# Transposing attention probabilities on VectorE and by DMA instead of on TensorE, in two stages of a four-layer kernel

## The chip, the cores and the metric

The kernel runs on one core of a Trainium2 chip. The core has five engines with an instruction queue each: TensorE (in the profile PE, with its weight loads as PEld), VectorE (DVE), ScalarE (ACT), GpSimd (POOL) and SyncE (SP), which here does nothing but issue DMAs. Sixteen DMA engines move the data. An engine takes its instructions in order, and an instruction whose operands are not ready holds up all that is queued behind it on that engine. The metric is device time in microseconds (us) for one launch of the whole kernel.

## The reference, cut to what matters

The program is four transformer layers on 1024 tokens of width 256, each an attention and a feed-forward part. The change touches the second and the fourth attention (L1 and L3 in the names of the inputs, `attn1` and `attn3` in the kernel). Both compute, for 16 heads of width 128 and in float32:

```
q, k, v = projections of x                      # L1: 16 heads each; L3: 16 query heads, 4 key/value heads
                                                # L3 also normalizes each q and k row by its mean square
s = q @ k.T * scale                             # 1024 x 1024 scores of a head
s = where(col <= row, s, -inf)                  # causal
p = softmax(s)
out = concat over heads (p @ v) @ Wo            # added to x, then normalized
```

The feed-forward part of the third layer (L2) has weights packed in 4 bits. The kernel unpacks them while `attn1` runs, and that unpacking is touched as well.

## The kernel before, in words

**Blocks.** The 1024 tokens are 8 blocks of P = 128. A *unit* is one head and one block of 128 queries. With the causal mask, query block j needs key blocks 0 to j, so a unit has 1 to 8 blocks of 128 keys, 4.5 on average. Each of the two attentions has 128 units and 576 squares of 128 x 128 probabilities.

**The loops.** `attn1` goes over four groups g of four heads, in a group over the heads h, in a head over half (0, 1) and s (0 to 3): the units of a head have 1, 2, ... 8 blocks. `attn3` goes over four groups g, in a group over the query block b (0 to 7), in a block over the four heads h: four units of equal size follow each other. Between units both stages work off a list of `pieces`, which are the projections that make queries, keys and values of this group and the next; in the last group few or none are left.

**A unit's way through the engines.** `scores` (L277) multiplies queries by keys on TensorE (L281) into a PSUM tile called `wide`, of which there are two. `exp_scores` (L237) adds the mask to the last 128 columns on VectorE (L241), takes the maximum of the row on VectorE (L246; in `attn3` one more small multiplication, L248) and the exponential on ScalarE with the sum of the row beside it (L251). `norm_probs` (L257) inverts the sum on VectorE (L258) and scales the row on GpSimd (L259). `transpose_probs` (L261) transposes each 128 x 128 square on TensorE into a PSUM bank (L268), and ScalarE copies up to four squares at a time to the SBUF tiles `pt` (L272). The product with the values, in `attend` (L1042 in `attn1`, L1934 in `attn3`), takes a value block as the stationary side and 512 columns of `pt`, that is four units, as the moving side (L1047, L1937). VectorE copies its result out (L1054, L1944), and the output projection follows (L1032 in `attn1`, L701 in `attn3`).

**The order around the change.** Both stages run under `in_order` (L140): PE, ACT, DVE and POOL execute their instructions in the order in which the Python code emits them. SP is not among these, so its DMAs go out as soon as a buffer is free. The order is made by `Pipe.advance` (L394), which is called once for each new unit i. It emits, in this order: `norm_probs` of unit i-1; what stands in `k.later` (GpSimd operations of the unpacking); `scores` of unit i; `transpose_probs` of unit i-2; `exp_scores` of unit i; then one step of the products with values that are due. `Pipe.then` (L390) makes a product due three calls after its last unit was handed in. After that the stage's loop emits pieces and a step of the unpacking.

**Buffers.** `SCOPES` (L2033) gives the number of buffers of each pool: in `attn1` three for the exponentials (`p4`) and three for the transposed (`pt`, 128 x 4 x 512), in `attn3` three and four. PSUM has eight banks; two `wide` tiles take four, the rest is the pool `bank`.

**Loads.** `load(g)` in `attn1` (L949) issues the weights of the next group at the second unit of a group, in `attn3` (L1759) at its fifth. `ffn2_weights` (L1680) loads packed weights and scales on SP (L1690 to L1704), unpacks them on VectorE in steps (`dequantize`, L1640; L1651 is its first operation) and on GpSimd (L1672, L1673), and stores the result on SP (L1711).

Of the kernel before, what the change touches and what calls it, by code (L numbers as in the profile page):

```python
# [31 lines left out]
P = 128  # L32
T = 1024
NT = T // P
D = 256
# [7 lines left out]
class Kit:  # L43
# [96 lines left out]
    def in_order(self):  # L140

        e = mybir.EngineType
        return self.tc.manual_schedule(engines={e.PE, e.Activation, e.DVE, e.Pool})
# [117 lines left out]
    def transpose_probs(self, probs, blocks, pts, slot):  # L261


        for lo in range(0, blocks, 4):
            n = min(4, blocks - lo)
            ps = self.bank()
            for i in range(n):
                self.nc.tensor.transpose(  # L268
                    ps[:, i * P : (i + 1) * P],
                    probs[:, (lo + i) * P : (lo + i + 1) * P], self.ident,  # L270
                )
            self.nc.scalar.copy(  # L272
                pts[lo // 4][:, :n, slot * P : (slot + 1) * P],
                ps[:, : n * P].rearrange("p (b q) -> p b q", b=n),
            )

# [101 lines left out]
class Pipe:  # L378
# [3 lines left out]


    def __init__(self, k):
        self.k, self.first, self.second, self.rest, self.queued = k, None, None, [], []

    def unit(self, query, key, blocks, pts, slot, scale=None):
        self.advance((query, key, blocks, pts, slot, scale))
# [5 lines left out]
    def advance(self, new=None):  # L394
        k = self.k
        if self.first:
            k.norm_probs(*self.first[:3])
        k.catch_up()
        if new:
            query, key, blocks, pts, slot, scale = new  # L400
            sc = k.scores(query, key, blocks * P)
        if self.second:
            probs, n, _, pts_, slot_ = self.second
            k.transpose_probs(probs, n // P, pts_, slot_)
        self.second = self.first
        self.first = None
        if new:
            probs, inv = k.exp_scores(sc, blocks * P, scale)
            self.first = (probs, blocks * P, inv, pts, slot)
# [4 lines left out]
        while self.rest and next(self.rest[0], self) is self:  # L414
            self.rest.pop(0)

    def busy(self):
        return self.first or self.second or self.queued or self.rest
# [518 lines left out]
def attn1(k, a):  # L937


    nc = k.nc  # L940
    scale = 1.0 / math.sqrt(128)
# [7 lines left out]
    def load(g):  # L949
        cols = slice(g * 512, (g + 1) * 512)  # L950
        wk, wv = (
            k.weights([P, NC, 512], a[n][:, cols].rearrange("(c p) f -> p c f", p=P))
# [1182 lines left out]
```

## Time and profile before

| what | value |
|---|---|
| median of three runs | 2349.58 us (2348.33 to 2350.21) |
| profiled execution, its own time | 2349.2 us |
| its span, first to last instruction | 2347.5 us |
| granted TensorE clock, mean | 0.976 of full speed |
| window of the second attention's units | about 441 to 960 us, then its last output projections |
| window of the fourth attention's units | about 1480 to 1966 us |
| VectorE transposes, copies from SBUF to SBUF by SP in these windows | none |

The page gives for each engine the busy time, a share of the span and a count of instructions. Busy time is an average over eight stages, so the two attentions are looked at in windows of their own. The chain of work that ended last is followed backwards from the last instruction; what a line has of it is time that the line really set. In the groups of instructions a row reads: line, engine, operation, written tile <- read tiles, shapes, count | busy us, mean ns of one | idle time of the engine before them, and what ended it. A line number is that of the code printed above.

### The profile page before, as it was taken

The page shows a single profiled execution, that of the slowest core. Times are in us where ns is not written, and L with a number is a line of the kernel's source. Part 1 is how long each engine was busy: PE and PEld are TensorE (multiplying, and loading weights), DVE is VectorE, ACT ScalarE, POOL GpSimd, SP SyncE. Part 2 cuts the span into 40 slices and gives each one's busy share as a digit, 9 for nine tenths or more (in the row PEclk, how much of TensorE's full clock was granted, in tenths as well). Part 3 has the DMA queues.
Part 4 walks back from the last instruction along what each step waited for, and adds up shares of the span by engine and source line. Part 5 has one row for each costly group of instructions (what it writes and reads, how often), then busy time and mean ns, then how long its engine had stood idle before and what let it go on. Part 6 is the DMA issues. An engine that isn't in the chain of part 4 may idle for free.

```text
span 2347.5 us, 25446 instructions
## 1 busy us (share of the span) xinstructions
PE 2168.4 (92%) x8563; PEld 1222.0 (52%) x8563; DVE 1228.8 (52%) x2799; ACT 913.7 (39%) x2358; POOL 492.8 (21%) x637
## 2 busy tenths in 40 slices
PE   7999768899999999988898999899999999999997
PEld 4666544566656665754444444455555554444443
DVE  5677556565655646555773445544445575222223
ACT  3666524434343435444453223454445442111111
POOL 4333221322222323321110000332222221000000
PEclk9999979999999999989999999999999999999998
DMA  5100163110111101013200001000000000101100
GB/s 169 35 12 25 44 198 111 38 49 24 46 36 59 45 29 40 19 54 97 76 2 10 27 28 45 9 1 19 1 18 10 10 1 18 36 28 54 30 1 18
DMA packets 59346, 92.24 MB, mean 39 GB/s; under 512 B 9072, under 2 KB 33712, under 8 KB 59216
## 3 DMA queue, kind: packets, MB, share of 16 engines
q1 hardware_dynamic: 54304, 78.15, 10.4%
q0 software_dynamic: 4912, 12.46, 1.9%
q8 instruction: 69, 1.13, 0.2%
q14 instruction: 61, 0.50, 0.1%
HBM read 69.76 MB, written 17.17 MB: 37 GB/s over the span
## 4 chain that ended last, share of the span: by engine, by line
PE 68%; issue 11%; DVE 10%; ACT 6%; DMA 2%; POOL 1%; SPq 1%; DVEq 0%; ACTq 0%; POOLq 0%
PE bank L152 18%; PE wide L281 9%; PE bank L1047 5%; PE wide L306 5%; PE bank L268 5%; PE bank L1937 4%; PE bank L159 3%; ACT e L635 3%; PE bank L701 3%; PE bank L1032 2%; PE bank L1464 1%; PE bank L881 1%; PE bank L1202 1%; DVE st L627 1%; PE bank L690 1%
## 5 line engine op out<-in xcount | busy, mean ns | idle before, releaser
L152 PE MATMUL bank<-xT,w 128*128 128x512 f32 (+2 forms) x1520 | 659.0, 563 | 3.5 <-DVE xT L178 2.6
L152 PEld LDWEIGHTS bank<-xT,w 128*128 128x128 f32 (+1 forms) x1520 | 285.7, 193 | 279.9 <-issue 256.0
L259 POOL TENSOR_SCALAR p<-p,st 128x128 f32<-128x128 f32 (+7 forms) x256 | 190.9, 746 | 672.5 <-DVE st L258 530.9
L272 ACT COPY pt<-bank 128x512 f32<-128x512 f32 (+3 forms) x384 | 171.0, 480 | 316.4 <-PE bank L268 313.4
L281 PE MATMUL wide<-k,q 128*128 128x512 f32 (+3 forms) x768 | 290.6, 487 | 3.7 <-ACT p L251 2.8
L281 PEld LDWEIGHTS wide<-k,q 128*128 128x128 f32 x768 | 142.1, 190 | 136.6 <-issue 121.3
L246 DVE TENSOR_REDUCE st<-wide 128x1 f32<-128x128 f32 (+7 forms) x256 | 194.1, 758 | 13.5 <-DVE wide L241 0.5
L306 PE MATMUL wide<-t,w 128*128 128x512 f32 (+1 forms) x392 | 188.5, 603 | 4.9 <-DVE t L2026 3.2
L268 PE MATMUL bank<-ident,p 128*128 128x128 f32 x1152 | 169.3, 274 | 21.4 <-POOL p L259 20.0
L268 PEld LDWEIGHTS bank<-ident,p 128*128 128x128 f32 x1152 | 137.7, 141 | 85.6 <-issue 39.0
L2025 DVE TENSOR_TENSOR t<-t,bank 128x512 f32<-128x512 f32 (+1 forms) x66 | 45.4, 687 | 249.5 <-PE bank L152 248.9
L2024 ACT ACTIVATE t<-bank 128x512 f32<-128x512 f32 (+1 forms) x66 | 39.4, 597 | 315.1 <-PE bank L152 315.1
L241 DVE TENSOR_TENSOR wide<-wide,causal 128x128 f32<-128x128 f32 x256 | 74.7, 292 | 125.9 <-PE wide L281 124.8
L1047 PE MATMUL bank<-pt,v 128*128 128x512 f32 (+3 forms) x384 | 139.4, 487 | 0.0
L1937 PE MATMUL bank<-pt,v 128*128 128x512 f32 x288 | 137.4, 596 | 0.0
L251 ACT ACTIVATE p<-wide,st,factor 128x128 f32<-128x128 f32 (+7 forms) x128 | 106.4, 831 | 73.7 <-DVE st L248 73.0
L306 PEld LDWEIGHTS wide<-t,w 128*128 128x128 f32 (+1 forms) x392 | 68.3, 189 | 109.4 <-issue 48.0
L159 PE MATMUL bank<-w,xT 128*128 128x512 f32 (+3 forms) x320 | 122.8, 521 | 1.7 <-DVE xT L178 0.9
L251 ACT ACTIVATE p<-wide,st 128x128 f32<-128x128 f32 (+7 forms) x128 | 95.0, 742 | 65.2 <-DVE st L246 64.6
L635 ACT ACTIVATE e<-wide,st 128x128 f32<-128x128 f32 x256 | 89.8, 377 | 51.4 <-DVE st L627 36.2
L1489 ACT ACTIVATE pt<-wide 128x1024 f32<-128x1024 f32 (+3 forms) x96 | 75.6, 810 | 70.4 <-PE wide L1483 68.6
L233 DVE TENSOR_TENSOR x<-bank,x 128x256 f32<-128x256 f32 x120 | 49.6, 422 | 92.6 <-PE bank L1032 34.5
(309 smaller groups left out, 3066.7 us busy)
## 6 DMA issues: line engine op xcount, KB each, us to landing
w<-in_L_ffn_gate_up_dram SPq DMA_DIRECT2D x16, 512.0 KB
w<-in_L_attn_Wq_dram SPq DMA_DIRECT2D x12, 512.0 KB
w<-in_L_attn_Wo_dram SPq DMA_DIRECT2D x12, 512.0 KB
rows<-parts SPq DMA_DIRECT2D x16, 256.0 KB
w<-in_L_ffn_down_dram SPq DMA_DIRECT2D x8, 512.0 KB
w<-in_L_attn_Wk_dram SPq DMA_DIRECT2D x7, 512.0 KB
w<-in_L_attn_Wv_dram SPq DMA_DIRECT2D x6, 512.0 KB
moe_results<-y SPq DMA_DIRECT2D x23, 128.0 KB
```

Source lines behind the costliest of these rows:

```text
L152: self.nc.tensor.matmul(out, lhsT=weight(c), rhs=self.xcols(c, lo, n), start=c == 0, stop=c == NC - 1)
L159: self.nc.tensor.matmul(out, lhsT=self.xcols(c, lo, n), rhs=weight(c), start=c == 0, stop=c == NC - 1)
L246: nc.vector.tensor_reduce(top, scores[:, :n], axis=AX.X, op=ALU.max, negate=True)
L251: nc.scalar.activation(probs[:, :n], scores[:, :n], AF.Exp, bias=top, scale=1.0 if scale is None else scale, accum_out=total,)
L259: self.nc.gpsimd.tensor_scalar(probs[:, :n], probs[:, :n], total, 1.0, ALU.mult, ALU.mult)
L268: self.nc.tensor.transpose(ps[:, i * P : (i + 1) * P], probs[:, (lo + i) * P : (lo + i + 1) * P], self.ident,)
L272: self.nc.scalar.copy(pts[lo // 4][:, :n, slot * P : (slot + 1) * P], ps[:, : n * P].rearrange("p (b q) -> p b q", b=n),)
L281: self.nc.tensor.matmul(s[:, lo : lo + m], lhsT=query, rhs=key(lo, m), start=True, stop=True)
L306: nc.tensor.matmul(acc[m][:, half * HALF : (half + 1) * HALF], lhsT=down[:, m * P : (m + 1) * P], rhs=h, start=i == 0, stop=i == count - 1,)
L635: nc.scalar.activation(e[:, r, f, b, :], sc[:, r, f, b, :], AF.Exp, bias=top[:, at : at + 1], accum_out=total[:, at : at + 1],)
L1047: nc.tensor.matmul(out[:, lo:], lhsT=values[g, b][:, h * P : (h + 1) * P], rhs=pts[b // 4][:, b % 4, lo:], start=b == 0, stop=b == 4 * hal ...
L1937: nc.tensor.matmul(out, lhsT=values[i][:, g * P : (g + 1) * P], rhs=pts[i // 4][:, i % 4, :], start=i == 0, stop=i == b,)
```

## The change

The transposition is done in two steps without TensorE and PSUM. VectorE transposes squares of 32 x 32 within a row of partitions: `turn_probs` is one VectorE instruction for a whole unit, which reads the probabilities with a step of four elements (16 bytes) and writes densely into a new pool `turned` (two buffers). Four DMAs on SP, one for each 32 partitions of queries, then move rows of 128 to 1024 bytes from `turned` to their partitions in `pt`. What lands in `pt` has the 128 keys of a block on partitions, permuted consistently, and the queries in eight segments of 32 for two units.

A `pt` tile now serves two units (a *pair*) instead of four. The product with the values therefore has 256 moving columns instead of 512, and twice as many matmuls; its result is copied out by ScalarE instead of VectorE. In `attn1` only the last block of a pair is cut to 128 columns.

`Pipe.advance` has one stage less: it emits `norm_probs` of unit i-1, `scores` and `exp_scores` of unit i, and then `turn_probs` of unit i-1. A product still becomes due three calls after its last unit; when two or more products are waiting, two of them get a step.

SP joins the engines whose order is the code's (`in_order(transfers=True)`). The load of the next group in `attn1` is spread over three units, eight units later than before. In `attn1` all queries are copied out of PSUM by ScalarE, where VectorE did it for groups 1 to 3 (L985). Loads and stores of the unpacking move from SP's queue to GpSimd's; that part of the code comes at the same place, and so the load of the next packed tile is issued in the same step as the first operation on it.

```diff
-    def in_order(self):
+    def in_order(self, transfers=False):
         e = mybir.EngineType
-        return self.tc.manual_schedule(engines={e.PE, e.Activation, e.DVE, e.Pool})
+        engines = {e.PE, e.Activation, e.DVE, e.Pool}
+        return self.tc.manual_schedule(engines=engines | {e.SP} if transfers else engines)
...
-    def transpose_probs(self, probs, blocks, pts, slot):
-        for lo in range(0, blocks, 4):
-            n = min(4, blocks - lo)
-            ps = self.bank()
-            for i in range(n):
-                self.nc.tensor.transpose(
-                    ps[:, i * P : (i + 1) * P],
-                    probs[:, (lo + i) * P : (lo + i + 1) * P], self.ident,
-                )
-            self.nc.scalar.copy(
-                pts[lo // 4][:, :n, slot * P : (slot + 1) * P],
-                ps[:, : n * P].rearrange("p (b q) -> p b q", b=n),
-            )
+    def turn_probs(self, probs, blocks, pt, slot):
+        nc = self.nc
+        n = blocks * P
+        turned = self.tile("turned", [P, 2 * HALF])
+        nc.vector.transpose(
+            turned[:, :n].rearrange("p (b k q) -> p b k q", b=4, q=32),
+            probs[:, :n].rearrange("p (k i b) -> p b k i", b=4, i=32),
+        )
+        for a in range(4):
+            nc.sync.dma_start(
+                out=pt[:, slot * 4 + a, : blocks * 32],
+                in_=turned[a * 32 : a * 32 + 32, :n].rearrange("i (b r) -> i b r", b=4),
+            )
+    def probs_tile(self, blocks):
+        n = 4 if blocks <= 4 else 8
+        return self.tile("pt", [P, 8, n * 32], tag=f"pt{n}", bufs=self.pt_bufs[n])
+    def values(self, out, value, pt, b, last, first=0):
+        self.nc.tensor.matmul(
+            out[:, first * P :].rearrange("p (s q) -> p s q", q=32), lhsT=value,
+            rhs=pt[:, first * 4 :, b * 32 : b * 32 + 32], start=b == 0, stop=last,
+        )
...
-    def unit(self, query, key, blocks, pts, slot, scale=None):
-        self.advance((query, key, blocks, pts, slot, scale))
+        self.k, self.first, self.rest, self.queued = k, None, [], []
+    def unit(self, query, key, blocks, pt, slot, scale=None):
+        self.advance((query, key, blocks, pt, slot, scale))
     def then(self, steps):
@@ -393,29 +408,28 @@
     def advance(self, new=None):
         k = self.k
-        if self.first:
-            k.norm_probs(*self.first[:3])
+        before, self.first = self.first, None
+        if before:
+            k.norm_probs(*before[:3])
         k.catch_up()
         if new:
-            query, key, blocks, pts, slot, scale = new
+            query, key, blocks, pt, slot, scale = new
             sc = k.scores(query, key, blocks * P)
-        if self.second:
-            probs, n, _, pts_, slot_ = self.second
-            k.transpose_probs(probs, n // P, pts_, slot_)
-        self.second = self.first
-        self.first = None
-        if new:
             probs, inv = k.exp_scores(sc, blocks * P, scale)
-            self.first = (probs, blocks * P, inv, pts, slot)
+            self.first = (probs, blocks * P, inv, pt, slot)
+        if before:
+            probs, n, _, pt, slot = before
+            k.turn_probs(probs, n // P, pt, slot)
         for q in self.queued:
             q[0] -= 1
         while self.queued and self.queued[0][0] <= 0:
             self.rest.append(self.queued.pop(0)[1])
-        while self.rest and next(self.rest[0], self) is self:
-            self.rest.pop(0)
+        for _ in range(min(2, len(self.rest))):
+            while self.rest and next(self.rest[0], self) is self:
+                self.rest.pop(0)
...
+    k.pt_bufs = {4: 2, 8: 2}
...
-        if g == 0:
-            nc.scalar.activation(
-                out, ps, AF.Identity, bias=scaled_bq[:, j : j + 1], scale=scale
-            )
-        else:
-            nc.vector.tensor_scalar(out, ps, bq[:, j : j + 1], scale, ALU.add, ALU.mult)
+        nc.scalar.activation(out, ps, AF.Identity, bias=scaled_bq[:, j : j + 1], scale=scale)
...
-    def attend(g, h, half, pts):
-        out = k.bank()
-        for b in range(4 * half + 4):
-            lo = max(0, b - 4 * half) * P
-            nc.tensor.matmul(
-                out[:, lo:], lhsT=values[g, b][:, h * P : (h + 1) * P],
-                rhs=pts[b // 4][:, b % 4, lo:], start=b == 0, stop=b == 4 * half + 3,
-            )
-            if b % 2:
+    def attend(g, h, half, pair, pt):
+        count = 4 * half + 2 * pair + 2
+        out = k.bank()[:, : 2 * P]
+        for b in range(count):
+            last = b == count - 1
+            k.values(out, values[g, b][:, h * P : (h + 1) * P], pt, b, last, int(last))
+            if b % 4 == 3 and not last:
                 yield
-        oT = outs[g, h, half] = k.tile("ot", [P, HALF])
-        nc.vector.tensor_copy(oT, out)
-        if h == 3:
+        if pair == 0:
+            outs[g, h, half] = k.tile("ot", [P, HALF])
+        nc.scalar.copy(outs[g, h, half][:, pair * 2 * P : (pair + 1) * 2 * P], out)
+        if (h, pair) == (3, 1):
+            yield
             yield from add_up(g, half)
...
-            if (h, half, s) == (0, 0, 1) and g < 3:
-                load(g + 1)
+            if (h, half) == (1, 0) and g < 3:
+                if s == 0:
+                    loading = load(g + 1)
+                next(loading, None)
             if s == 0:
                 ensure(make_queries, g, 15)
                 ensure(make_keys, g, h, half)
-                pts = [k.tile("pt", [P, 4, HALF]) for _ in range(half + 1)]
             blocks = 4 * half + s + 1
+            if s % 2 == 0:
+                pt = k.probs_tile(blocks + 1)
             pipe.unit(
                 queries[g][:, h, (blocks - 1) * P : blocks * P],
-                lambda lo, n: keys[g, h][:, lo : lo + n], blocks, pts, s,
+                lambda lo, n: keys[g, h][:, lo : lo + n], blocks, pt, s % 2,
             )
...
+                if not mine and pieces[0][0] is not make_queries and (h, half) < (1, 1):
+                    break
...
-            if s == 3:
-                ensure(make_values, g, 4 * half + 3)
-                pipe.then(attend(g, h, half, pts))
+            if s % 2:
+                ensure(make_values, g, 4 * half + s)
+                pipe.then(attend(g, h, half, s // 2, pt))
...
-                nc.sync.dma_start(out=packed, in_=a[f"L2_ffn_{n}_W_packed"][:, cols])
-                nc.sync.dma_start(
+                nc.gpsimd.dma_start(out=packed, in_=a[f"L2_ffn_{n}_W_packed"][:, cols])
+                nc.gpsimd.dma_start(
                     out=scales,
                     in_=a[f"L2_ffn_{n}_scales"][:, cols].unsqueeze(1).to_broadcast([8, 16, 512]),
                 )
...
-            nc.sync.dma_start(out=k.dequantized[-1], in_=out)
+            nc.gpsimd.dma_start(out=k.dequantized[-1], in_=out)
...
+    k.pt_bufs = {4: 2, 8: 4}
...
-    def attend(g, b, pts):
-        out = k.bank()
+    outs = {}
+    def attend(g, b, pair, pt):
+        out = k.bank()[:, : 2 * P]
         for i in range(b + 1):
-            nc.tensor.matmul(
-                out, lhsT=values[i][:, g * P : (g + 1) * P], rhs=pts[i // 4][:, i % 4, :],
-                start=i == 0, stop=i == b,
-            )
-            if i % 2:
+            k.values(out, values[i][:, g * P : (g + 1) * P], pt, i, i == b)
+            if i % 4 == 3 and i < b:
                 yield
-        oT = k.tile("ot", [P, HALF])
-        nc.vector.tensor_copy(oT, out)
+        if pair == 0:
+            outs[g, b] = k.tile("ot", [P, HALF])
+        oT = outs[g, b]
+        nc.scalar.copy(oT[:, pair * 2 * P : (pair + 1) * 2 * P], out)
+        if pair == 0:
+            return
         yield
         project_heads(k, b, oT, ws[g][1])
...
-    attn1: dict(q=2, k=5, v=12, pt=3, p4=3, ot=8, bv=1, prep=1),
+    attn1: dict(q=2, k=5, v=12, pt=2, p4=2, turned=2, ot=7, bv=1, prep=1),
...
-    attn3: dict(q=12, k=4, v=8, pt=4, p4=3, ot=3, t2=4, raw=2),
+    attn3: dict(q=12, k=4, v=8, pt=2, p4=2, turned=2, ot=3, t2=4, raw=2),
...
```

The split of `load` in `attn1` into a generator with a `yield` after each weight and the same calls in the loop of `attn3` are left out above.

## The prediction

> **What bounds the kernel now.** First the page: busy time and the chain.
>
> ```profile
> PE 2168.4 (92%) x8563; PEld 1222.0 (52%) x8563; DVE 1228.8 (52%) x2799; ACT 913.7 (39%) x2358; POOL 492.8 (21%) x637
> PE 68%; issue 11%; DVE 10%; ACT 6%; DMA 2%; POOL 1%; SPq 1%; DVEq 0%; ACTq 0%; POOLq 0%
> L272 ACT COPY pt<-bank 128x512 f32<-128x512 f32 (+3 forms) x384 | 171.0, 480 | 316.4 <-PE bank L268 313.4
> L268 PE MATMUL bank<-ident,p 128*128 128x128 f32 x1152 | 169.3, 274 | 21.4 <-POOL p L259 20.0
> ```
>
> TensorE bounds it. The 1152 transposes (L268) keep TensorE busy for 169.3 us, but matmuls overlap, so I ask the chain what they really set. I cut the units into stretches by where the mask addition (L241) starts: A, the first 13 heads of `attn1` (104 units, 441 to 885 us); B, its last three heads, almost without pieces (24 units, 885 to 960); C, groups 0 to 2 of `attn3` (96 units, 1480 to 1843); D, its last group (32 units, 1843 to 1966). The windows view gives the engines in A, B, C, D (columns: PE, PEld, DVE, ACT, POOL busy us and instructions):
>
> ```profile
> 441.00:885.00 444.00, 438.04 (x1697) 273.44 (x1696) 251.60 (x569) 175.10 (x393) 118.55 (x138) 1.00 0.12 40
> 885.00:960.00 75.00, 69.63 (x299) 44.27 (x298) 48.47 (x115) 38.15 (x89) 28.58 (x32) 1.00 0.11 36
> 1480.00:1843.00 363.00, 342.37 (x1325) 197.93 (x1324) 180.11 (x473) 175.60 (x405) 99.72 (x105) 0.99 0.03 9
> 1843.00:1966.00 123.00, 113.29 (x467) 69.17 (x466) 79.30 (x267) 54.23 (x123) 28.14 (x43) 1.00 0.02 5
> ```
>
> TensorE is busy 92 to 99% in each, VectorE 50 to 65%. The chain in each window gives L268 10.9, 10.6, 11.7 and 9.0%, that is 48.4, 8.0, 42.5 and 11.1 us: 110 us in all.
>
> **What goes.** The 1152 transposes leave TensorE: 110 us of chain, the most that this change can save there. ScalarE loses 171.0 us of copies (L272) and takes over 128 copies of 128x256 (about 375 ns each, the mean of L272 at that size: 48 us) and 48 query copies (696 ns, L981: 33 us); it has room, and I cost that at nothing. The values' columns are as many as before. A 256-column pass costs little more than half of a 512-column one (L1032: 16 passes in 3.46 us, so about 0.205 us each; 512 columns come every 0.43 us), so halving the passes is free. TensorE would need 395.6 + 67.0 + 320.5 + 111.9 = 895 us.
>
> **What VectorE gets.** 256 transposes of 128 to 1024 columns, 576 on average. No VectorE transpose is in this trace. From below: the maximum (L246) reads densely, 292 ns for 128 and 1225 ns for 1024 columns, so 0.16 us fixed and 1.04 ns a column. From above: L985 writes with a step of 64 bytes, beside L233 of the same size, dense:
>
> ```profile
> L985 DVE TENSOR_SCALAR q<-bank,bq 128x256 f32<-128x256 f32 x48 | 31.4, 655 | 41.1 <-PE bank L152 41.1
> L233 DVE TENSOR_TENSOR x<-bank,x 128x256 f32<-128x256 f32 x31 | 13.2, 425 | 33.9 <-PE bank L1032 33.9
> ```
>
> That is (655 - 159) / 256 = 1.94 ns a column. The new instruction reads with a step of 16 bytes, so I take the upper end. With 59.9, 13.8, 55.3 and 18.4 thousand columns the transposes cost 132.8, 30.6, 122.7 and 40.9 us (at the lower end 78.9, 18.2, 72.9, 24.3). Off go L985 (31.5 us, all in A) and the copies L1054 (16.3, 4.8) and L1944 (15.1, 6.9). VectorE then has 336.6, 74.3, 287.7 and 113.3 us. It waits in order between masks, exponentials and scaling, so I allow it nine tenths of a stretch (TensorE, which waits for less, reaches 92 to 99%): 374, 82.6, 319.7, 125.9. The larger of the two engines in each stretch: 395.6 + 82.6 + 320.5 + 125.9 = 925 us against 1005. **Saving 80 us**; B becomes slower, A and C gain.
>
> The Trainium skill speaks against this change: "VectorE: DVE Perf Modes", section "Rules for kernel authors", sends a 128x128 transpose to TensorE where PSUM will do as the target, and keeps VectorE's for 32x32. Its table has 311 ns for VectorE and 390 ns for TensorE on bf16; by it, 1152 squares would cost VectorE an estimated 358 us, near my 327, and TensorE 449 us, which this trace refutes (110 us of chain).
>
> **The transfers.** Four DMAs a unit on SP, 1024 in all. The nearest rows are four small SBUF-to-SBUF copies in the third attention, there and back:
>
> ```profile
> 1236.66 2.44 SPq L1509 DMA_DIRECT2D inv<-ot  x4
> 1240.44 0.25 DVE L1515 RECIPROCAL inv<-inv 128x16 f32<-128x16 f32 x1 [12.07 <-DMA inv<-ot]
> 1240.76 2.44 SPq L1517 DMA_DIRECT2D ot<-inv  x4
> 1244.48 1.10 PE L1524 MATMUL wide<-ot,pick 128*128 128x512 f32 x2 [1.42 <-DMA ot<-inv]
> ```
>
> Four issues take SP 2.44 us, and the reader starts 3.7 to 3.8 us after the first issue. SP needs 2.44 us a unit where a unit lasts 3.1 us (B) to 4.3 us (A): it keeps up. The page's queue q1 moved 54304 packets of 1439 bytes on average in 10.4% of 16 engines' span, 72 ns each; 512 rows a unit are at most 2.3 us of the 16 engines, and 0.9 us scaled to 576 bytes. So I take 4.3 us from a finished transpose to landed rows (3.8 and half a microsecond for longer rows). The ends are 3.8 and 6: in the chain one such copy, which met 256 KB stores, took 4.61 us from 1108.88, and three more have to be issued.
>
> Is that covered? From the scores of unit i, VectorE needs 0.29 + 0.75 (mean of L246) + 1.28 + about 0.5 (L248, waits) = 2.8 us to finish transposing unit i-1, then 4.3: 7.1 us. The product reads it in the call of unit i+2, two units of TensorE work later: 7.6 us in A, 5.6 in B, 6.7 in C, 7.0 in D. What is missing falls on every second pair only, since the product's wait also delays the scores after it: half of 1.5 us in B, of 0.4 in C, of 0.1 in D. B and D are set by VectorE anyway, C loses about 10 us at most, covered below. At 6 us it would be 8.8 us: half of 1.2, 2.1 and 1.8 in A, C, D over 52, 48, 16 pairs, 31 + 50 + 14 = 95 us, more than the gain; from about 5.1 us (7.9: half of 0.3 and 1.2 in A and C, 8 + 29 = 37 us) nothing is left.
>
> The page "DMA: Bandwidth & Descriptors", section "Rules for kernel authors", warns that transfers under 64 KB are mostly overhead, with some 2.0 us fixed for each; mine average 72 KB. One after another, four would be an estimated 8.7 us, which would undo the gain; the rows above show four within 3.8 us.
>
> **What else is added.**
> - Unpacking loads. Now the packed load is issued at 483.50 us and first used at 492.36: 9 us of lead. After, it comes in GpSimd's queue behind a store (0.6 to 0.7 us to issue, L103) and in the same step as L1651. GpSimd's DMAs land in 2.7 to 4.4 us; the transpose and a value copy ahead of L1651 hide some 2 us. VectorE stands 2 to 3 us for 12 tensors, with recip and mask of the next unit behind it. Two units in PSUM hide about half: 15 us (0 to 35).
> - Weight loads (9 in `attn1`, 6 in `attn3`, 512 KB) now share SP's order with the rows: 10 us (0 to 30).
> - A product waits for up to eight DMAs; L1524 spends 51 ns on each of two extra waits for four DMAs, so about 0.2 us for 128 products, half of it under running matmuls: 10 us (0 to 26).
> - At the end of each stage the last product waits out the longer way: 6 us.
>
> **Sum**: 2349.2 - 80 + 41 = **2310 us**. The profiled execution (2349.2) is 0.4 us below the median; that is left out.
>
> **Rivals.**
> 1. *All is hidden.* The transposes run at 1.04 ns a column; VectorE has 283, 62, 238 and 97 us, TensorE stays the bound at 895, half of the additions remain: 2349 - 110 + 20 = 2260. For it: a 16-byte step isn't 64. Against: L985.
> 2. *Slower: VectorE waits for GpSimd.* Before, TensorE took the scaled row two calls later; now VectorE, in order, stands for L259 in the same call, and all masks, maxima and evictions stand behind it. L259 takes 0.75 us on average, and in `attn1` unpacking (1.27 and 1.49 us each) and its DMA issues sit ahead of it. Between recip and transpose VectorE has 1.04 us of mask and maximum, which covers it in equal units. With x us exposed a unit, and 0.95 instead of 0.9 since the wait is counted: from x = 0.4 the stretches sum to 961, which with 41 is 1002, no gain; at x = 0.6, 420 + 93 + 364 + 140 = 1017, so 2349 + 12 + 41 = 2402, say 2400. A transpose at 2.3 ns a column would also use up the gain (398 + 88 + 342 + 133 = 961).
> 3. *The lag eats it.* Landing takes 5.1 us instead of 4.3: 2310 + 37 = 2347, say 2350. For it: the 4.61 us row; against: the two rows at 3.7 and 3.8.
>
> **Chances.** Forecast (2285 to 2340) 0.42; rival 1 0.20; rival 2 0.30; rival 3 0.08. Rival 3 gives a quarter to faster, half to no change (within 0.2%, about what a measurement of this kernel can tell), a quarter to slower: faster 0.64, same 0.04, slower 0.32. The range takes rival 1 and its bound (895 us and no additions: 2239) and rival 2 to its price: 2240 to 2400; the forecast's own is 2285 to 2340.
>
> **What would show it.** L268 and L272 gone; the transposes' mean at 576 columns near 1.28 us (rival 1: 0.76); VectorE busy near 85% in A and C, over 90% in B and D; B longer than 75 us; TensorE's waits put down to the copies into `pt` small. Rival 2 shows as VectorE idle before the transpose, released by L259; rival 3 as TensorE idle before the products, released by a DMA. I am wrong in the main step if TensorE's share in A and C falls below 85%.

## The result and the profile after

| | median of | us | ratio to the kernel before |
|---|---|---|---|
| before | 4 runs | 2348.95 (2345.68 to 2350.21) | |
| after | 4 runs | 2494.77 (2484.01 to 2497.36) | 1.0614 (95%: 1.058 to 1.0649) |

The forecast was 2310 us, range 2240 to 2400. The kernel became 6% slower: the time lies outside the range, and it moved the other way than forecast.

First the page of the kernel after: busy time, chain, and the groups of the product (L288) and of the new transpose (L271). A group reads: busy us, mean ns | idle time of the engine before it and what ended most of it.

```profile
PE 2132.5 (86%) x7955; PEld 1245.6 (50%) x7955; DVE 1439.0 (58%) x2943; ACT 817.5 (33%) x2150; POOL 516.0 (21%) x677
PE 51%; DVE 17%; issue 13%; DMA 7%; ACT 5%; SPq 4%; POOL 3%; DVEq 0%; ACTq 0%; POOLq 0%
L288 PE MATMUL bank<-pt,v 128*128 128x256 f32 x1216 | 333.4, 421 | 177.2 <-DMA pt<-turned 160.3
L288 PEld LDWEIGHTS bank<-pt,v 128*128 128x128 f32 x1216 | 255.5, 217 | 263.0 <-issue 173.0
L271 DVE STREAM_TRANSPOSE turned<-p 128x128 f32<-128x128 f32 (+7 forms) x256 | 311.7, 1218 | 65.9 <-DMA pt<-turned 39.7
```

TensorE lost work as planned, and its share still fell from 92 to 86%. It now stands before the products: 160.3 us until rows have landed, and the weight loads of the same line (PEld) stand 173.0 us at "issue", with 504 waits on semaphores of up to 5.7 us. In the chain, SP and DMA together grew from 3 to 11%, VectorE from 10 to 17%.

The windows view of the same stretches A, B, C, D (columns: window, its length, then PE, PEld, DVE, ACT, POOL busy us and instructions, granted clock, DMA share, GB/s):

```profile
439.00:935.00 496.00, 419.25 (x1442) 278.66 (x1441) 323.37 (x600) 152.23 (x338) 136.37 (x168) 0.93 0.41 99
935.00:1047.00 112.00, 74.07 (x234) 50.59 (x234) 70.47 (x135) 25.34 (x63) 33.16 (x40) 0.82 0.41 95
1571.00:1959.00 388.00, 323.11 (x1113) 203.23 (x1111) 267.07 (x545) 131.80 (x310) 99.99 (x105) 0.94 0.36 79
1959.00:2110.00 151.00, 110.51 (x395) 77.28 (x396) 111.08 (x292) 37.65 (x90) 28.14 (x43) 0.89 0.39 92
```

The stretches took 444, 75, 363 and 123 us; they take 496, 112, 388 and 151: 142 us more, of the 143 by which the two profiled spans differ. TensorE is busy 85, 66, 83 and 73%, VectorE 65, 63, 69 and 74%: **no engine is full**. The lost time is waiting between them. The granted clock, 0.99 to 1.00 here before, is 0.82 to 0.94.

One such wait, from the timeline around the end of a head (start, duration, engine, line; in brackets idle time and its releaser; not every line is shown):

```profile
855.24 1.80 DVE L271 STREAM_TRANSPOSE turned<-p 128x896 f32<-128x896 f32 x1
855.28 0.38 PE L297 MATMUL wide<-k,q 128*128 128x128 f32 x2
...
856.97 0.65 DVE L1016 TENSOR_TENSOR v<-bank,bv 128x512 f32<-128x512 f32 x1
857.53 0.41 DVE L1676 TENSOR_SCALAR c<-packed 128x512 int32<-128x512 int32 x1
857.98 0.69 DVE L1689 SCALAR_TENSOR_TENSOR v<-c,v 128x512 f32<-128x512 int32 x1
...
859.99 2.04 DVE L271 STREAM_TRANSPOSE turned<-p 128x1024 f32<-128x1024 f32 x1 [0.72 <-POOL p L261]
860.03 1.88 PE L161 MATMUL bank<-w,xT 128*128 128x512 f32 x4
...
861.75 0.81 PE L297 MATMUL wide<-k,q 128*128 128x384 f32 x2
...
866.82 3.40 PE L288 MATMUL bank<-pt,v 128*128 128x256 f32 x8 [4.26 <-DMA pt<-turned]
...
872.23 0.69 DVE L1016 TENSOR_TENSOR v<-bank,bv 128x512 f32<-128x512 f32 x1 [4.79 <-PE bank L161]
```

The transpose of an 8-block unit ends at 862.03, and its product starts 4.8 us later. I had 4.3 for that step, so the way of the rows was sized nearly right. The other two figures of the comparison are to be read here as well. From the scores of the next unit (855.28) VectorE took 6.75 us to finish this transpose, where I had 2.8: the transpose of 7 blocks, a value copy (L1016) and two operations of the unpacking stood ahead in its order, it waited 0.72 us for GpSimd, and this is the *largest* transpose. On TensorE's side the units that follow are the first of the next head, with 1, 2 and 3 blocks. Their scores are done at 862.56, 7.3 us after 855.28, and next in its order is the product. Then VectorE waits 4.79 us in turn.

### The profile page after: what moved, and what is told of

Its sections match the earlier page's. It is cut to its first block, busy times and chain, and to the rows that moved or that the text cites. A ratio compares the mean times of both kernels' runs of the same rounds, so it can differ in the third digit from the quotient of the medians.

```text
span 2490.8 us, 25898 instructions
## 1 busy us (share of the span) xinstructions
PE 2132.5 (86%) x7955; PEld 1245.6 (50%) x7955; DVE 1439.0 (58%) x2943; ACT 817.5 (33%) x2150; POOL 516.0 (21%) x677
## 3 DMA queue, kind: packets, MB, share of 16 engines
q8 instruction: 65, 1.06, 0.2%
## 4 chain that ended last, share of the span: by engine, by line
PE 51%; DVE 17%; issue 13%; DMA 7%; ACT 5%; SPq 4%; POOL 3%; DVEq 0%; ACTq 0%; POOLq 0%
PE bank L154 15%; PE bank L288 7%; DMA pt<-turned 5%; PE wide L297 5%; DVE turned L271 5%; PE wide L322 5%; SPq L276 3%; PE bank L161 3%; ACT e L649 3%; PE bank L1047 2%; DVE st L248 2%; PE bank L715 1%; PE bank L1485 1%; POOL p L261 1%; DVE st L641 1%
## 5 line engine op out<-in xcount | busy, mean ns | idle before, releaser
L288 PE MATMUL bank<-pt,v 128*128 128x256 f32 x1216 | 333.4, 421 | 177.2 <-DMA pt<-turned 160.3
L288 PEld LDWEIGHTS bank<-pt,v 128*128 128x128 f32 x1216 | 255.5, 217 | 263.0 <-issue 173.0
L271 DVE STREAM_TRANSPOSE turned<-p 128x128 f32<-128x128 f32 (+7 forms) x256 | 311.7, 1218 | 65.9 <-DMA pt<-turned 39.7
L297 PE MATMUL wide<-k,q 128*128 128x512 f32 (+3 forms) x768 | 302.0, 508 | 4.3 <-ACT p L253 3.1
L297 PEld LDWEIGHTS wide<-k,q 128*128 128x128 f32 x768 | 148.4, 200 | 127.6 <-issue 103.4
L248 DVE TENSOR_REDUCE st<-wide 128x1 f32<-128x128 f32 (+7 forms) x256 | 194.0, 758 | 8.8
L161 PEld LDWEIGHTS bank<-w,xT 128*128 128x128 f32 x320 | 60.7, 212 | 47.8 <-issue 42.7
L715 PE MATMUL bank<-w,ot 128*128 128x256 f32 x256 | 68.6, 408 | 12.0 <-ACT ot L1968 12.0
```

What stands on the lines that cost most here:

```text
L161: self.nc.tensor.matmul(out, lhsT=self.xcols(c, lo, n), rhs=weight(c), start=c == 0, stop=c == NC - 1)
L248: nc.vector.tensor_reduce(top, scores[:, :n], axis=AX.X, op=ALU.max, negate=True)
L271: nc.vector.transpose(turned[:, :n].rearrange("p (b k q) -> p b k q", b=4, q=32), probs[:, :n].rearrange("p (k i b) -> p b k i", b=4, i=32),)
L288: self.nc.tensor.matmul(out[:, first * P :].rearrange("p (s q) -> p s q", q=32), lhsT=value, rhs=pt[:, first * 4 :, b * 32 : b * 32 + 32], ...
L297: self.nc.tensor.matmul(s[:, lo : lo + m], lhsT=query, rhs=key(lo, m), start=True, stop=True)
L715: k.nc.tensor.matmul(y, lhsT=oT[:, h * P : (h + 1) * P], rhs=wo[:, h, :], start=h == 0, stop=h == 3)
```

## The experiments

The theory after the result, called the lag: the rows land too late for a product that is due three calls later, where transposes are large and the calls that follow have little work for TensorE. Rivals: VectorE's rate (transposes at some 1.9 ns a column hold the rows back), and the unpacking's late loads. All ratios are to the kernel before, measured again beside each group of runs, with 95% intervals. For several kernels the table gives the time in us from the first mask addition of a stretch to that of the next (for B and D to their own last one, so what follows their last unit is missing):

| kernel | A | B | C | D |
|---|---|---|---|---|
| before | 444.1 | 64.4 | 363.2 | 102.9 |
| after | 495.6 | 100.5 | 388.3 | 130.3 |
| e1, products later | 448.0 | 82.2 | 350.3 | 123.6 |
| e2, no transfers | 427.8 | 75.9 | 337.1 | 114.0 |
| e11, later, dense, loads early | 417.0 | 73.0 | 339.8 | 113.1 |
| e13, the same, no transfers | 393.5 | 61.8 | 329.5 | 103.5 |

**Products due later (e1).**

```diff
-        self.queued.append([3, steps])
+        self.queued.append([self.k.due, steps])
...
-    k.pt_bufs = {4: 2, 8: 2}
+    k.pt_bufs, k.due = {4: 2, 8: 2}, 5
...
-    k.pt_bufs = {4: 2, 8: 4}
+    k.pt_bufs, k.due = {4: 3, 8: 3}, 4
```

> The product with the values becomes due five calls after its last unit in attn1 and four in attn3, instead of three; in attn3 the buffers for the moved probabilities become three small and three large instead of two and four (SBUF has no more room). Nothing is left out. Theory L (lag): the way VectorE, SP, DMA, back to TensorE is longer than the two units it is given, in places where these units are small; then most of TensorE's idle time before the products (192 us put down to the DMAs and 186 us to issue) goes, and the time falls to 2350 to 2400 us. Theory V (rate): VectorE, with 312 us of transposes, is what holds the two stages up, and a later product changes nothing it has to do; then the time stays at 2460 us or more.

2376.84 us, ratio 1.012 (1.0094 to 1.0146): 118 of the 146 us are gone, with every transpose, transfer and queue as in the changed kernel. The same groups of its page:

```profile
L288 PE MATMUL bank<-pt,v 128*128 128x256 f32 x1216 | 294.9, 384 | 22.3 <-DMA pt<-turned 21.7
L288 PEld LDWEIGHTS bank<-pt,v 128*128 128x128 f32 x1216 | 239.0, 201 | 86.9 <-issue 40.9
L271 DVE STREAM_TRANSPOSE turned<-p 128x128 f32<-128x128 f32 (+7 forms) x256 | 312.6, 1221 | 95.0 <-DMA pt<-turned 70.7
L297 PE MATMUL wide<-k,q 128*128 128x512 f32 (+3 forms) x768 | 315.7, 523 | 70.9 <-ACT p L253 68.7
```

TensorE's wait for rows fell from 160.3 to 21.7 us. A part of the waiting has moved. VectorE waits 70.7 us, in the changed kernel 39.7, to get one of its two `turned` buffers back. And TensorE waits 68.7 us before the scores (L297), there 3.1, until an exponential frees one of the two `wide` tiles; before the exponentials of `attn1`, ScalarE waits 335.0 us for VectorE's maxima (L248).

**No transfers (e2).** VectorE writes its squares straight into `pt`:

```diff
-        turned = self.tile("turned", [P, 2 * HALF])
         nc.vector.transpose(
-            turned[:, :n].rearrange("p (b k q) -> p b k q", b=4, q=32),
+            pt[:, slot * 4 : slot * 4 + 4, : blocks * 32].rearrange("p b (k q) -> p b k q", q=32),
...
-        for a in range(4):
-            nc.sync.dma_start(
-                out=pt[:, slot * 4 + a, : blocks * 32],
-                in_=turned[a * 32 : a * 32 + 32, :n].rearrange("i (b r) -> i b r", b=4),
-            )
```

> VectorE writes the 32x32 squares straight into the tile that the products read; the 1024 DMAs that bring them to their partitions are left out, so the products multiply misplaced probabilities. VectorE's transposes stay. Theory L: the way back to TensorE is shorter by about 4.8 us (end of the transpose to start of the product, as in the profile after), and the time falls to 2290 to 2350 us. Theory V: only the 40 us in which VectorE waits for a free buffer go; 2420 us or more.

2328.04 us, ratio 0.9921 (0.9904 to 0.9938). The transfers cost 167 us in this kernel. But 2328 is also well above what my sum gives without them, so they are not the only error; more on that below.

**Dense reads (e3).** The transpose reads without the step of 16 bytes, which puts the keys in another order:

```diff
-            probs[:, :n].rearrange("p (k i b) -> p b k i", b=4, i=32),
+            probs[:, :n].rearrange("p (k b i) -> p b k i", b=4, i=32),
```

> VectorE reads the probabilities densely instead of with a step of 16 bytes; the keys of a block then arrive in another order than the values have them, so the products are of misordered keys. All else stays. If the step costs the second cycle, the transposes fall from 1218 ns to about 760 ns on average, 312 to 195 us in sum. Theory L: the lag shortens by 0.5 us on average, 0.9 us for the largest units; 2430 to 2465 us. Theory V: about 100 us less, 2390 us.

2429.62 us, ratio 1.0352 (1.0319 to 1.0385): 65 of the 146 us are gone, and 113 us of the transposes' time.

```profile
L288 PE MATMUL bank<-pt,v 128*128 128x256 f32 x1216 | 312.6, 401 | 148.2 <-DMA pt<-turned 125.2
L271 DVE STREAM_TRANSPOSE turned<-p 128x128 f32<-128x128 f32 (+7 forms) x256 | 198.3, 775 | 62.9 <-DMA pt<-turned 31.4
```

The wait for rows is still 125.2 us, where the changed kernel has 160.3. The time is at the lower edge of the range of the lag theory and 40 us above that of VectorE's rate alone. The two aren't quite apart: a faster transpose also shortens the lag, since its rows leave sooner.

**Packed weights loaded early (e4), and with the later products (e5).** The packed tile is loaded as soon as its only buffer is read for the last time, instead of in the same step as the first use of the new one:

```diff
-def dequantize(k, packed, scales, out):
+def dequantize(k, packed, scales, out, then):
...
         bits(8)
+        if i:
+            then()
         yield
```

> The next packed tile of the unpacking is loaded right after the last read of the one before, three to four units ahead of its first use, instead of in the same step. Nothing is left out. In the profile after, VectorE stands 18 us before L1676 for these loads. Both theories: 10 to 25 us less, 2470 to 2485 us. A third theory U, that these 12 stalls set off most of the loss in attn1 (88 us): 2430 us or less.

2483.39 us, ratio 1.0563 (1.0537 to 1.0589): 11 us less. VectorE's idle time before L1676 was 36.8 us in the changed kernel (the 18 us of the expectation are those of one of three kinds of tensor); it is gone here, and less than a third of it came off the time. The theory of late loads is out as a main cause.

> Both edits together: the later products (five calls in attn1, four in attn3) and the packed loads of the unpacking ahead of their first use. Alone they gave 2377 and 2483 us. With the later products VectorE still stands 54 us before L1676 in attn1, 11 times some 5 us. Theory R1, that these stalls are now most of what is left over the kernel before: 2325 to 2345 us. Theory R2, that the round trip of the moved rows (67 us in which VectorE waits for a free buffer) is what is left: 2365 us or more.

2363.06 us, ratio 1.005 (1.0033 to 1.0068): 14 us below e1, less than was hoped: 18 us above the range of R1 and 2 below that of R2. VectorE's wait for `turned` is now 91.7 us, so the packed loads were not what held the rows.

**Two of four DMAs issued by ScalarE: with products later (e6) and at the change's own distance (e9).**

```diff
-            nc.sync.dma_start(
+            (nc.scalar if a % 2 else nc.sync).dma_start(
```

> The later products (2377 us alone), and two of the four DMAs of a unit are issued by ScalarE's queue instead of SP's. Nothing is left out. Four issues on SP take 4 x 0.6 = 2.4 us; split they take 1.2 us, so buffers come free 1.2 us earlier. R2: 2335 to 2358 us. R1: within 8 us of 2377. Third theory: ScalarE, in order, now waits for the transpose ahead of the next exponential and spends 1.2 us a unit on issuing; slower than 2385 us.

2453.62 us, ratio 1.0442 (1.0424 to 1.0461): 77 us *slower* than e1.

> The changed kernel with products due after three calls, as it was, and two of the four DMAs of each unit issued by ScalarE's queue. Theory L (lag): the way back is 1.2 us shorter, against 4.8 us removed with the transfers (2328 us, 167 less); about a quarter of that, 2435 to 2460 us. If the issue time on SP doesn't count, since the DMA's own latency is the whole lag: 2480 us or more.

2491.42 us, ratio 1.0614 (1.0591 to 1.0637): no gain. The trace of e6 at the line of the DMAs (duration in ns: shortest, median, longest), the group of the product, and TensorE's waits for one of ScalarE's copies (us in total, times, longest) in e1 and in e6:

```profile
L276 ACTq DMA_DIRECT2D pt<-turned x512: 550/618/1923, 445.1 to 2057.8; - x171
```

```profile
L288 PE MATMUL bank<-pt,v 128*128 128x256 f32 x1216 | 299.0, 389 | 5.3 <-DMA pt<-turned 5.3
```

```profile
PE bank L715 <- ACT ot L1968: 7.9, 9, 1.5
PE bank L715 <- ACT ot L1968: 58.0, 27, 4.7
```

The products hardly wait for rows, but ScalarE issues 512 DMAs at a median of 618 ns, that is 316 us, in one order with its other work, and stands in that order until each transpose is done. What this holds up is above all ScalarE's copies of finished products (`ot`, L1968 and L1069): TensorE's waits for them rose from 9.1 us in e1 to 82.4, near the 77 us lost, while its wait for exponentials fell from 68.7 to 61.3. In e9 the same trade comes out even: the wait for rows fell from 160.3 to 123.0 us, the one for L1968 rose from 12.0 to 52.3.

**Products later and no transfers (e7).** The edits of e1 and e2.

> The later products without the 1024 DMAs (the products multiply misplaced probabilities). It shows how much of the 2377 us is still due to the transfers once products are late enough, and what distance alone is worth without them (2328 us with products due after three calls). R1: the packed loads still stall VectorE, the transfers no longer matter; 2350 us or more. R2: 2310 to 2330 us.

2322.91 us, ratio 0.988 (0.9859 to 0.99), 5 us from e2. Without transfers the distance is worth next to nothing: what e1 won was the transfers' lag, and 54 us of transfers were left in e1.

**Dense reads with the right result (e8).** The keys' columns are put in the new order when ScalarE writes them from PSUM, the causal mask likewise; with the edits of e1 and e3.

```diff
         nc.scalar.activation(
-            keys[g, h][:, half * HALF : (half + 1) * HALF], ps, AF.Identity,
-            bias=bk[:, at : at + 1],
+            keys[g, h][:, half * HALF : (half + 1) * HALF].rearrange(
+                "p (k b i) -> p k b i", b=4, i=32
+            ),
+            ps.rearrange("p (k i b) -> p k b i", b=4, i=32), AF.Identity, bias=bk[:, at : at + 1],
```

> With the products due 5 and 4 calls later 2376.8 us were measured; without the transfers as well 2322.9. This kernel keeps all transfers and the distance, but lets the transposes read densely: the keys' columns are put in another order when they are written (and the causal mask with them), so that the result is the same. That takes some 0.8 ns a column, about 110 us, off VectorE's busy time. If VectorE's rate is what still holds the transposes' rows back, 2310 to 2335. If the transfers themselves (their landing, and the two buffers that a transpose has to get back from them) are what is left, 2355 or more; ScalarE's key evictions with a step of 16 bytes, should they be slower, would come on top.

2339.2 us, ratio 0.996 (0.994 to 0.998): 38 us below e1, 4 us above the range for VectorE's rate and 16 below that of its rival.

**All three (e11), a call later still (e12), all three without transfers (e13).** e11 has the edits of e5 and e8; e13 that of e2 as well. e12 is e11 with

```diff
-    k.pt_bufs, k.due = {4: 2, 8: 2}, 5
+    k.pt_bufs, k.due = {4: 2, 8: 2}, 6
...
-    k.pt_bufs, k.due = {4: 3, 8: 3}, 4
+    k.pt_bufs, k.due = {4: 4, 8: 3}, 5
```

> As the run before it in this batch (distance and dense reads), and the packed int4 weights are loaded as soon as their buffer is read for the last time. Distance with early loads alone was 2363.1. If VectorE's rate is what is left: 2300 to 2330, faster than the kernel before the change. If the transfers are: 2345 to 2365.

2314.08 us, ratio **0.9862 (0.9842 to 0.9882)**: 1.4% below the kernel before, with an interval clear of 1, and 25 us below e8, from the early loads alone.

```profile
L293 PE MATMUL bank<-pt,v 128*128 128x256 f32 x1216 | 290.7, 380 | 33.5 <-DMA pt<-turned 28.1
L276 DVE STREAM_TRANSPOSE turned<-p 128x128 f32<-128x128 f32 (+7 forms) x256 | 198.6, 776 | 136.4 <-DMA pt<-turned 102.5
```

> Distance, dense reads and early loads, with the products one call later still: due 6 calls later in the second attention and 5 in the fourth (buffers 4 and 3 there). If what is left is a lag that more distance would cover, 8 to 20 us below the same kernel at 5 and 4. If what is left is the order in which transposes wait for two buffers and SP issues, the same within 6 us, or slower, since a product holds its probabilities longer.

2320.53 us, ratio 0.9879 (0.9851 to 0.9906): its interval overlaps that of e11, so still more distance showed no gain.

> Distance, dense reads and early loads, without the transfers: VectorE writes its transposed squares straight into the tile that the products read, so the probabilities of most keys stand on wrong partitions and the output is not the reference's. It is the floor of this form of the work. Due 5 and 4 without transfers was 2322.9 with a step of 16 bytes in the read. If VectorE is still a bound there, 2285 to 2305; if TensorE alone sets the pace, 2310 to 2325.

2255.16 us, ratio 0.96 (0.9579 to 0.962), below both ranges. Here, by the windows view, TensorE is at last full in A:

```profile
441.00:835.00 394.00, 390.15 (x1443) 261.48 (x1444) 281.29 (x600) 149.43 (x337) 138.05 (x169) 1.00 0.14 45
```

So e11's transfers still cost 59 us, although the products come later.

**What of the transfers is left: weight loads out (e16), on GpSimd's queue (e17), out of the changed kernel (e18).** Left out with the weights in e16 and e18 are three loads of value biases (256 KB each). The edit in `attn1`; `attn3` has the like:

```diff
-                    loading = load(g + 1)
+                    ws[g + 1], loading = ws[0], iter(())
```

> The kernel with distance, dense reads and early packed loads (2314.1), without the weight loads of groups 1 to 3 in the second and fourth attention: these groups use the first group's weights, so the output is not the reference's. In its profile 48 of the 102 us in which VectorE waits for a buffer that its rows have not left yet fall within 20 us after such loads. If rows queue behind the weights: 2280 to 2300, and VectorE's wait for these buffers falls to some 55 us. If these waits would only come elsewhere (SP's issue rate at small units, or VectorE idle anyway): 2308 to 2316.

2293.52 us, ratio 0.9765 (0.9748 to 0.9781): 21 us less. VectorE's waits in e16 (us in total, times, longest):

```profile
DVE turned L276 <- DMA pt<-turned: 84.6, 71, 5.0
```

That is less than e11's 102.5, but not the 55 that were expected: part of the waits comes elsewhere.

```diff
-        self.nc.sync.dma_start(out=t, in_=source)
+        (queue or self.nc.sync).dma_start(out=t, in_=source)
```

> The same kernel with all its work; the weight loads of groups 1 to 3 in both stages are issued by GpSimd, so they are in another queue than the rows. If the rows wait because they are behind the weights in one queue, most of what leaving the loads out gives: 2290 to 2305. If they wait because the 16 DMA engines are busy with 512 KB, no matter from which queue, 2310 to 2320; GpSimd's issues in front of its row scalings may cost some more.

2319.93 us, ratio 0.9875 (0.9858 to 0.9891): no gain over e11, and VectorE's wait for `turned` is 107.0 us (e11: 102.5). Another queue doesn't help, so it fits that 512 KB loads take the DMA engines from the rows, not that rows stand behind them in order; GpSimd's own issues could hide a small gain.

> The changed kernel itself, without the weight loads of groups 1 to 3 in both stages (these groups use the first group's weights, so the output is not the reference's). The prediction put the weight loads that share SP's order at 10 us (0 to 30). If that was right: 2465 to 2495. If the weights in the rows' queue are a main part of the 59 us in which the transfers hold the best version back, and a lag of three calls covers less of it than one of five: 2430 to 2465.

2478.88 us, ratio 1.0563 (1.0546 to 1.0581): 16 us, near the 10 that I had. **Left open**: the other 38 of the 59 us. Candidates are SP's issue rate (four issues at a median of 602 ns, 2.4 us, against units that follow each other in 1.6 to 2.2 us at the start of a group of `attn3` in e11) and the two `turned` buffers. A third one was not tried.

## Why the prediction was wrong, step by step

The forecast was 185 us too low. Without any transfers my sum was 2349.2 - 80 + 15 = 2284, and e2 measured 2328: 44 us. The transfers were to cost 26 (weights 10, semaphores 10, stage ends 6), and cost 167: 141 us. For the lag itself, "C loses about 10 us at most, covered below", the sum has no term.

**1. "Is that covered?" failed: most of the 141 us.** That step set 2.8 us of VectorE and 4.3 us of rows against TensorE's mean work of two units, 5.6 to 7.6 us. The rows were sized nearly right. From the page's DMA issues (KB each, median us from issue to landing):

```profile
pt<-turned SPq DMA_DIRECT2D x128, 128.0 KB, 2.7
pt<-turned SPq DMA_DIRECT2D x128, 64.0 KB, 2.1
```

Three issues at 602 ns ahead of the last one make 1.8 us, so an 8-block unit takes 4.5 us; the timeline shows 4.8. The term that was furthest off is VectorE's 2.8 us. It starts with the mask, as if VectorE were free when the scores come, and takes the mean transpose. Of the 124 products for which the trace gives all three figures, TensorE stood more than 0.3 us before 55, 167 us in sum. There VectorE took 5.1 us in the median from the start of the next unit's scores to the finished transpose, the rows 4.8 until the product started, and TensorE's work until the product's turn was 6.4 us. That about every second pair waits was right.

The worst place is the end of a head in `attn1`, where sizes run from 1 to 8 blocks: the slowest transposes (up to 2056 ns), one behind the other on VectorE, meet the units with the least work. At the 12 of these products that waited, 61 us in sum, VectorE took 7.0 us in the median, the rows 5.1, and TensorE's work was 6.6 us. In 11 of the 16 heads the interval after the third unit is 6.7 to 9.9 us, where before it was 2.1 to 4.5 in all. Among the five without it are the very first head, which follows no other, and the first heads of groups 1 to 3, where an output projection and pieces of the next group stand ahead of the product. And a wait isn't only its own length: VectorE stands behind TensorE (4.79 us above), and the next rows are late too.

e1 shows that it was the comparison of delay and cover: with nothing else changed but the distance and the number of `pt` buffers, 118 us came back. How much each of the three figures has of that was not measured by a run of its own; e3, whose transposes are shorter at the same distance, gave 65.

**2. "The larger of the two engines in each stretch" failed: 44 us.** It gave 395.6 us for A and 320.5 for C. Without transfers (e2) they still took 427.8 and 337.1, with VectorE 75 and 77% busy, not the nine tenths that I allowed. The windows of e2, A and C:

```profile
439.00:867.00 428.00, 402.36 (x1454) 265.81 (x1452) 321.23 (x601) 150.22 (x338) 137.25 (x169) 0.98 0.13 41
1465.00:1802.00 337.00, 306.14 (x1113) 195.25 (x1112) 258.89 (x545) 130.29 (x310) 100.27 (x105) 0.97 0.03 10
```

A maximum over a whole stretch lets a busy moment of the one engine be repaid in an idle moment of the other; with unequal units and two buffers between the engines, it isn't. The page of e2 shows TensorE waiting for VectorE all the same, through the exponentials and directly:

```profile
L291 PE MATMUL wide<-k,q 128*128 128x512 f32 (+3 forms) x768 | 300.6, 506 | 36.9 <-ACT p L253 35.8
L282 PE MATMUL bank<-pt,v 128*128 128x256 f32 x1216 | 294.1, 384 | 13.5 <-DVE pt L270 12.2
```

That is 50 us, where the same two groups had 4 before (L281 3.7; L1047 and L1937 nothing). That unequal units are the reason is argued. Only in e13, at 1.06 ns a column, do A and C come near the forecast, 393.5 and 329.5. From e7 to e13 are 68 us, by dense reads and early loads together; the early loads by themselves gave 11 to 25 (e4, e5, e8 to e11), so VectorE's rate is the larger part, though not measured alone there.

**3. What TensorE loses** (110 us of chain) was not measured by itself. Rival 1's price, 2260 for transposes at 1.04 ns and nothing exposed, is near e13's 2255; but e13 has no transfers at all and three edits more, so this is no test of it. The change itself met neither condition.

**4. The transposes' rate was right**: 327 us forecast at 1.94 ns a column, 311.7 measured, (2056 - 390) / 896 = 1.86 ns. L985 was the nearer row.

**5. Unpacking loads**, 15 us: 11 (e4), 14 (from e1 to e5) and 25 (from e8 to e11). I took GpSimd's DMAs to land in 2.7 to 4.4 us; the page before also has two rows of 5.7, and in the changed kernel these loads took 5.2 to 8.3. **Weight loads**, 10 us: 16 (e18). Semaphores and stage ends were not measured by themselves.

**6. Rival 2** (VectorE waits for GpSimd) is out. The group of the transpose with all that ended its waits:

```profile
L271 DVE STREAM_TRANSPOSE turned<-p 128x128 f32<-128x128 f32 (+7 forms) x256 | 311.7, 1218 | 65.9 <-DMA pt<-turned 39.7 <-POOL p L261 19.4 <-POOL t L1842 1.2
```

19.4 us in 256 units is 0.08 us a unit, where 0.4 would have decided.

**7. Rival 3 named the mechanism** (the lag eats the gain), but only for rows that land later than 5.1 us; I gave it 0.08, and its price stood on the same means. In 35 of the 55 waiting cases the rows took less than that, so what ate the gain was the lag as a whole and not mainly a longer landing. The sign that I had set against the main step, TensorE below 85% in A and C, came: 84.5 and 83.3%. VectorE's share, forecast near 85% in A and C and over 90% in B and D, was 65, 69, 63 and 74%.

The rule of the Trainium skill that I weighed and set aside ("VectorE: DVE Perf Modes", section "Rules for kernel authors", a 128x128 transpose goes to TensorE) advised rightly for this kernel as it was changed. What the runs add is where the loss arose: not in the instruction's price, which I had right, but in the way to the reader, from the engine that transposes late to the rows that land late. With that way covered, dense reads and early packed loads, e11 is 1.4% faster than the kernel with TensorE's transposes.

## What to carry to other kernels

When a step of a software pipeline gets longer, don't hold its delay against the mean work between producer and consumer: walk through the sequence of units and look at the place where the largest producer is followed by the smallest work. Count there, too, what stands ahead of the producer in its engine's order. Cover was cheap to add here (two numbers and a different split of the buffers gave back 118 us), so a change that lengthens a path should move its consumer in the same edit. And a layout that costs a step in the read of one engine may be free elsewhere: try it in a copy that is made anyway.

## What the runs showed of the hardware

- **VectorE's transpose** of squares of 32 takes 300 ns for 128 and 1247 ns for 1024 columns when it reads densely, 1.06 ns a column; with a step of 16 bytes 390 and 2056 ns, 1.86 ns. The Trainium skill, "SBUF — State Buffer", section "Door 1: The DMA port swizzle (why `[64,N]` ≈ `[32,N]`)", says that each access which crosses to a new 16-byte line pays a penalty; this step crosses at every element, and the runs agree. ScalarE read PSUM with the same step for nothing: its key copies take 687 ns in e11 and 685 ns in the kernel after.
- **The clock falls with the waits.** In A to D of the changed kernel TensorE is busy 85, 66, 83 and 73% of the time, and the granted clock is 0.93, 0.82, 0.94 and 0.89. In B it was 1.00 before; in A of e13, where TensorE is full, it is 1.00 again. Matmuls of the product take 421 ns on average after and 371 in e13. The Trainium skill, "TensorE: Matmul & The Clock Gate", section "Why this matters for your kernels", warns of idle gaps of over some 3 us; the waits here last up to 7.6 us. So a wait seems to cost more than its length, which my sum left out; no run separates the two.
- **Landing time of the rows is not constant**: median 1.8 us (16 KB) to 2.7 us (128 KB), and up to 8.6 us.
- **Issuing from ScalarE** cost it 618 ns of its queue for each DMA (median). With the copies of finished products in the same order, that undid more than half of what the distance had won (e6: 77 of 118 us).
